# Norm scale and shift by two token tiles on GpSimd, and pieces of other work in any step

## The chip, the cores and the metric

The kernel runs on one core of one Trainium2 chip. A core has five engines that matter here: TensorE (matrix products; PE in the profile), VectorE (DVE), ScalarE (ACT), GpSimd (POOL), and SyncE (SP), which issues the transfers (DMA). Each engine works through its own queue of instructions in order and waits on semaphores for what others produce. The metric is the device time of one execution in microseconds (us), and lower is better.

## The reference, cut to what matters

Sixteen sequences of 1024 nodes with 128 features pass three graph transformer layers and then one graph attention layer. All share one 1024 x 1024 adjacency matrix.

```python
# layers 0 to 2, for each of 16 sequences
Q, K, V = x @ Wq, x @ Wk, x @ Wv                      # 8 heads of 16
scores = where(adj == 0, -inf, Q K^T / 4)             # 1024 x 1024 for each head
x = layer_norm(x + softmax(scores) V @ Wo + bo, ln1_g, ln1_b)
y = relu(x @ W1 + b1) @ W2 + b2                       # 128 -> 256 -> 128
x = layer_norm(x + y, ln2_g, ln2_b)
# layer 3
h = x @ W
e = leaky_relu((h @ a_src)[:, None] + (h @ a_dst)[None, :], 0.2)
out = layer_norm(softmax(where(adj == 0, -inf, e)) @ h + x, ln_gamma, ln_beta)
```

`layer_norm` ends in `... * g + b`: the scale and the shift that the change is about.

## The kernel before

The kernel handles 48 blocks (16 sequences by 3 layers), four sequences side by side, so that while one sequence's attention runs, the rest of another's layer is computed. A block has 32 steps: two groups of four heads, two halves of the queries, and eight tiles of keys (`kt`). A step computes the scores of four heads, as two pairs, against 128 keys; exponentiates and masks them; and four steps later (`AHEAD`) multiplies them with the values. One pair is always masked on VectorE, before the exponential (`mask_add`). The other is masked on GpSimd after it (`mask01`), except in the steps where `kt` is 2, 5 or 7: there VectorE masks both.

```python
LANES = 4
FEW = 20
AHEAD = 4
BOTH_ON_DVE = (2, 5, 7)
...
            on_pool = pp == 0 and kt not in BOTH_ON_DVE
            m = (mask01 if on_pool else mask_add)[:, kt, q0:q0 + 512][:, None, :].to_broadcast([P, 2, 512])
            if on_pool:
                nc.scalar.activation(ev, psv, AF.Exp, scale=HD ** -0.5)
                behind["pool"] = nc.gpsimd.tensor_mul(ev, ev, m).ins
            else:
                behind["dve"] = nc.vector.tensor_add(ev, psv, m).ins
                masked.append((2 * step_no[0] + pp + (kt not in BOTH_ON_DVE), ev))
```

All other work is cut into pieces. The projections of the next block are 8 pieces, what follows attention (output projection, norms, feed-forward) is 11, and the last layer of a sequence is 12. They stand in queues ("chains"), each with a least distance in steps from the piece ahead of it, and at most one is taken after a step, by `piece()`. `need(mark)` takes pieces at once until a given one is done.

```python
    def piece():
        few = sum(len(c["queue"]) for c in chains) < FEW and now[0] < (len(blocks) - LANES) * 4 * NT
        if few and now[0] % NT in BOTH_ON_DVE:
            return
        for chain in chains:
            if now[0] >= chain["due"] + chain["queue"][0][0] and take(chain):
                return
...
                if m + 1 < len(blocks):
                    if at == 6:
                        need(("post",) + (blocks[m + 1][0], blocks[m + 1][1] - 1) if blocks[m + 1][1] else
                             ("fetch", blocks[m + 1][0]))
                        put(proj_tasks(m + 1), ("proj", m + 1), first=True)
                    if at == 24:
                        need(("proj", m + 1))
                        stack(m + 1, 0)
```

`stack` copies keys and queries by DMA into the layout that the scores need. The norms: VectorE sums and takes the statistics (`stats`), and GpSimd normalises and then scales and shifts.

```python
    def normalise(n, ts):
        z, _, mv = n
        m, v = mv[:, ts, 0], mv[:, ts, 1]
        nc.gpsimd.tensor_scalar(m, m, -1.0, None, op0=OP.mult)
        nc.gpsimd.tensor_scalar(v, v, EPS, None, op0=OP.add)
        nc.gpsimd.tensor_tensor(v, v, half_neg[:, ts], OP.pow)
        for t in range(ts.start, ts.stop):
            nc.gpsimd.tensor_scalar(z[:, t, :], z[:, t, :], mv[:, t, 0:1], mv[:, t, 1:2], op0=OP.add, op1=OP.mult)

    def scale_shift(z, gain, bias):
        n = z.shape[1]
        nc.gpsimd.tensor_mul(z, z, rows(gain, n))
        nc.gpsimd.tensor_add(z, z, rows(bias, n))
```

When the half of the queries that is being summed ends, `finish` transposes the one accumulator on VectorE (`tt`), and GpSimd divides by the sums (`A`); the piece `both` transposes `A` on VectorE (`aT`).

```python
            with soon():
                nc.vector.transpose(tt.rearrange("p a b -> p (a b)"), acc)
            rec = state["recs"][:, g, qh, :]
            nc.vector.reciprocal(rec, tt[:, :, HD])
            nc.gpsimd.tensor_mul(state["A"][:, qh, :, g, :], tt[:, :, :HD],
                                 rec[:, :, None].to_broadcast([P, 16, HD]))
```

In the main loop the order on TensorE and ScalarE is that of the program; on VectorE and GpSimd a scheduler sets it when the kernel is built.

Of the kernel before, what the change touches and what calls it, by code (L numbers as in the profile page):

```python
# [28 lines left out]
SOON = 120  # L29
LANES = 4  # L30
FIRST = 1
FEW = 20
AHEAD = 4
BOTH_ON_DVE = (2, 5, 7)
TILES = {"w": 10, "x": LANES + 1, "last": 2}
# [77 lines left out]
def fast_path(ctx: ExitStack, tc: tile.TileContext, a: dict, out: bass.AP, flag):  # L113
    nc = tc.nc
    x_dram, adj = a["x"], a["adj"]
    B, N, D = x_dram.shape
    NT = N // P
# [40 lines left out]
    def fetch(b):  # L158
        def run():
            state["x", b] = load_x(b)  # L160
        return run
# [30 lines left out]
    def neighbours(t):  # L192
        ai, ab = rows_in[t]
        nc.vector.tensor_scalar(ab, ai, 0.0, None, op0=OP.not_equal)

    def mask_rows(t):
        ab = rows_in[t][1]
        ps = slot(BF16)
        for k in range(NT):
            nc.tensor.transpose(ps[:, k * P:(k + 1) * P], ab[:, k * P:(k + 1) * P], identb)  # L200
        return ps

    def masks(t, ps):
        psv = ps.rearrange("p (k q) -> p k q", q=P)
        nc.vector.tensor_copy(mask01[:, :, t * P:(t + 1) * P], psv)
        nc.scalar.activation(mask_add[:, :, t * P:(t + 1) * P], psv, AF.Identity, scale=-BLOCKED, bias=blocked,
                             saturate=False)
# [14 lines left out]
    def first_weights():  # L222
        W[0].update(load_layer(nc, nc.sync, const, a, 0, ("Wo", "b2", "W1", "b1", "W2", "ln1_g", "ln2_g")))
        norm_weights(nc.sync, 0)
# [5 lines left out]
    def other_weights():  # L230
        for l in range(1, L):
            W.append(load_layer(nc, nc.sync, const, a, l, [n for n in LAYER if n not in ("ln1_b", "ln2_b")]))
            norm_weights(nc.sync, l)
        nc.sync.dma_start(ln2_b_last, rows_of(a[f"L{L - 1}_gnn_ln2_b"]))
        for n in LAST:
            src = a[f"L3_gnn_{n}"]
            if n == "W":
                t = w_nodes[:, :D]
                nc.sync.dma_start(t, src)
            elif n in ("a_src", "a_dst"):  # L240
                t = const.tile([P, 1], F32, name=n)
                nc.sync.dma_start(t, src.rearrange("(p o) -> p o", o=1))
            else:
                t = const.tile([P, D], F32, name=n)
                nc.sync.dma_start(t, rows_of(src))
            wl[n] = t

    def biases():
        for l in range(L):
            if l:  # L250
                add_bias(nc.sync, "ln2_b", l - 1, "bo", l)
            add_bias(nc.sync, "ln1_b", l, "b2", l)

    def last_weights():
        a2 = const.tile([P, 2], F32)
        nc.vector.tensor_copy(a2[:, 0:1], wl["a_src"])
        nc.vector.tensor_copy(a2[:, 1:2], wl["a_dst"])
        ps = bank()
        nc.tensor.transpose(ps[:, :P], w_nodes[:, :D], identf)
        w3t = work.tile([P, P], F32, tag="row", name="w3t", bufs=2)  # L260
        nc.vector.tensor_copy(w3t, ps[:, :P])
        ps = bank()
        nc.tensor.matmul(ps[:, :2], w3t, a2, start=True, stop=True)
        nc.vector.tensor_copy(w_nodes[:, D:], ps[:, :2])
# [3 lines left out]
    for i in range(2):  # L268
        t = const.tile([P, NT, H, HD + 1], F32, name=f"v{i}")
# [29 lines left out]
    def rows(v, n=NT):  # L299
        return v[:, None, :].to_broadcast([P, n, D])  # L300
# [37 lines left out]
            nc.gpsimd.tensor_scalar(z[:, t, :], z[:, t, :], mv[:, t, 0:1], mv[:, t, 1:2], op0=OP.add, op1=OP.mult)  # L338

    def scale_shift(z, gain, bias):  # L340
        n = z.shape[1]
        nc.gpsimd.tensor_mul(z, z, rows(gain, n))  # L342
        nc.gpsimd.tensor_add(z, z, rows(bias, n))

    checks = [0]

# [51 lines left out]
    def stack(m, g):  # L398

        for pp in range(2):  # L400
            for n, order in (("Wk", (0, 1, 0, 1)), ("Wq", (0, 0, 1, 1))):
                t = work.tile([P, N], F32R, tag=n, name=n, bufs=4)
                r0 = (g * J + 2 * pp) * HD
                for i, part in enumerate(order):
                    behind["stack"] = nc.sync.dma_start(t[i:P:4, :].bitcast(F32), state[n, m][part][r0:r0 + 2 * HD, :].bitcast(F32)).ins
                state[n, g, pp] = t
# [245 lines left out]
    blocks = [(b, l) for p in range(0, B, LANES) for l in range(L) for b in range(p, p + LANES)]  # L652
    chains = []
    done = {("fetch", b) for b in range(2)}
    now = [0]
# [3 lines left out]
    def put(tasks, mark, chain=None, first=False):  # L659

        if chain is None:
            chain = {"due": now[0], "queue": deque()}
            chains.insert(0 if first else len(chains), chain)
        for n, task in enumerate(tasks):
            chain["queue"].append(task + (mark if n == len(tasks) - 1 else None,))
        return chain

    def take(chain):

        gap, f, tiles, mark = chain["queue"][0]  # L670
        if any(free[t[1:]] == 0 for t in tiles.split() if t[0] == "+"):
            return False
        chain["queue"].popleft()
        f()
        for t in tiles.split():
            free[t[1:]] += -1 if t[0] == "+" else 1
        done.add(mark)
        chain["due"] = now[0]
        if not chain["queue"]:
            chains.remove(chain)  # L680
        return True

    def piece():
        few = sum(len(c["queue"]) for c in chains) < FEW and now[0] < (len(blocks) - LANES) * 4 * NT
        if few and now[0] % NT in BOTH_ON_DVE:
            return
        for chain in chains:
            if now[0] >= chain["due"] + chain["queue"][0][0] and take(chain):
                return

    def need(mark):
        while mark not in done:
            first = next(c for c in chains if any(q[3] == mark for q in c["queue"]))
            assert take(first) or any(take(c) for c in list(chains) if c is not first)
# [62 lines left out]
    n = 0  # L757
    with tc.manual_schedule(engines={mybir.EngineType.PE, mybir.EngineType.Activation}):
        for m, (b, l) in enumerate(blocks):
            order = [(g, qh) for g in range(G) for qh in range(2)]  # L760
            if m in (0, len(blocks) - 1):
                order.sort(key=lambda x: x[1])
            for at, (g, qh, kt) in enumerate((g, qh, kt) for g, qh in order for kt in range(NT)):
                now[0] = n
                if at == (6 if m == 0 else 1):
                    stack(m, 1)
                if n == 6:
                    with tc.issue_after(behind["stack"]):
                        first_weights()
                        other_weights()  # L770
                if n == 20:
                    with tc.issue_after(behind["pool"]):
                        biases()
                if n == 40:
                    with tc.issue_after(behind["dve"]):
                        last_weights()
                if at == 0 and m + 2 < len(blocks) and blocks[m + 2][1] == 0:
                    put([(0, fetch(blocks[m + 2][0]), "+x")], ("fetch", blocks[m + 2][0]))
                if m + 1 < len(blocks):
                    if at == 6:  # L780
                        need(("post",) + (blocks[m + 1][0], blocks[m + 1][1] - 1) if blocks[m + 1][1] else
                             ("fetch", blocks[m + 1][0]))
                        put(proj_tasks(m + 1), ("proj", m + 1), first=True)
                    if at == 24:
                        need(("proj", m + 1))
                        stack(m + 1, 0)
                step = m, g, qh, kt
                if FIRST <= n < FIRST + 4:

                    with tc.manual_schedule(engines={mybir.EngineType.DVE}):  # L790
                        e = score_step(step)
                        neighbours(4 + n - FIRST)
                        masks(4 + n - FIRST, mask_rows(4 + n - FIRST))
                else:
                    e = score_step(step)
                waiting.append((step, e, n + AHEAD))
                av_due(n)
                piece()
                n += 1
        exponentials(0)  # L800
        for n in range(n, n + 2 * AHEAD):
            now[0] = n
            av_due(n)
            piece()
        while chains:
            now[0] += 1
            for chain in list(chains):
                if now[0] >= chain["due"] + chain["queue"][0][0]:
                    take(chain)
# [236 lines left out]
```

## Time and profile before

| | before |
|---|---|
| time, median of 3 | 4098.15 us (4097.01 to 4099.05) |
| span of the profiled execution | 4095.1 us |
| TensorE busy, granted clock | 3818.2 us, 0.98 |
| VectorE, ScalarE, GpSimd busy | 3393.5, 3381.9, 3450.5 us |
| GpSimd: mask product, 128 x 1024 (L428) | 960 of 2153 ns |
| GpSimd: scale, 128 x 1024 (L342) | 95 of 2394 ns |
| GpSimd: scale, 128 x 512 (L342) | 34 of some 1287 ns |

The profile shows one execution. Its page gives the busy time of each engine, the chain of work that ended last, and groups of instructions by source line. A group's row has the line, the engine, the operation, what it writes and reads, its shape and count, then its busy time in us and the mean of one in ns, then how long the engine idled just before it and what ended most of that. Busy times of engines that work side by side don't add up to the span.

### The profile page before, as it was taken

The numbers are of one execution on the slowest core, as the hardware profiler recorded it, in microseconds if no ns is written. First come the engines' busy times: TensorE is split into PE (matmuls) and PEld (weight loads), VectorE is DVE, ScalarE is ACT, GpSimd is POOL, SyncE is SP. The second block draws the span as 40 slices with busy tenths as digits, with TensorE's granted clock in tenths as the row PEclk, the third lists the DMA queues.
The fourth block names the chain that finished last, engine by engine and source line by source line (L and its number), as shares of the span: only waits on it lengthen the run. The fifth ranks groups of instructions, "written<-read, shape, count | busy, mean of one in ns | idle before, by whom it ended". The sixth has DMA issues, their size and how long they took to land.

```text
span 4095.1 us, 107716 instructions
## 1 busy us (share of the span) xinstructions
PE 3818.2 (93%) x44501; PEld 1548.0 (38%) x44501; DVE 3393.5 (83%) x5326; ACT 3381.9 (83%) x3961; POOL 3450.5 (84%) x3010
## 2 busy tenths in 40 slices
PE   7999999999999999999999999999999999999986
PEld 2333333344443333334444333333444433333445
DVE  7888888888788888888878888888888788888873
ACT  7999999977778999897777989998777798988760
POOL 5888988978878989898877989898887789998884
PEclk8999999999999999999999999999999999999997
DMA  6222122122222222122222222121222122221200
GB/s 160 61 63 58 47 63 63 42 62 54 58 54 63 50 63 63 43 64 54 53 54 62 54 63 59 46 63 43 74 54 54 48 63 52 54 63 42 62 12 17
DMA packets 124465, 233.13 MB, mean 57 GB/s; under 512 B 34624, under 2 KB 73792, under 8 KB 123968
## 3 DMA queue, kind: packets, MB, share of 16 engines
q1 hardware_dynamic: 122960, 225.71, 21.9%
q8 instruction: 354, 5.80, 0.6%
q14 instruction: 143, 1.17, 0.1%
q10 hardware_dynamic: 1008, 0.44, 0.1%
HBM read 15.54 MB, written 8.39 MB: 6 GB/s over the span
## 4 chain that ended last, share of the span: by engine, by line
PE 43%; DVE 21%; POOL 14%; ACT 14%; issue 6%; SPq 0%; DMA 0%; ACTq 0%; DVEq 0%; POOLq 0%
PE t L294 17%; PE acc L447 14%; DVE e L430 12%; PE s L420 11%; ACT e L442 7%; POOL e L428 7%; ACT e L427 4%; POOL x L338 3%; DVE st L319 2%; POOL mv L336 2%; DVE lo L383 2%; PE t L283 1%; DVE tt L458 1%; ACT hT L503 1%; POOL x L342 1%
## 5 line engine op out<-in xcount | busy, mean ns | idle before, releaser
L430 DVE TENSOR_TENSOR e<-s,mask_add 128x1024 f32<-128x1024 f32 x2112 | 2490.4, 1211 | 363.6 <-PE s L420 311.2
L442 ACT ACTIVATE e<-e 128x1024 f32<-128x1024 f32 x2112 | 2209.7, 1070 | 404.1 <-DVE e L430 385.0
L428 POOL TENSOR_TENSOR e<-e,mask 128x1024 f32<-128x1024 f32 x960 | 2052.8, 2153 | 322.7 <-ACT e L427 308.9
L447 PE MATMUL acc<-e,v 128*17 128x512 f32 x12288 | 1628.8, 602 | 49.4 <-DVE tt L458 22.2
L420 PE MATMUL s<-Wq,Wk 64*128 64x512 f32 x6144 | 1206.1, 459 | 90.1 <-DVE e L430 62.6
L427 ACT ACTIVATE e<-s 128x1024 f32<-128x1024 f32 x960 | 990.7, 1032 | 157.2 <-PE s L420 150.3
L420 PEld LDWEIGHTS s<-Wq,Wk 64*128 64x128 f32 x6144 | 501.6, 185 | 1078.1 <-DVE e L430 422.1
L447 PEld LDWEIGHTS acc<-e,v 128*17 128x17 f32 x12288 | 207.3, 95 | 556.4 <-issue 406.4
L338 POOL TENSOR_SCALAR x<-x,mv 128x128 f32<-128x128 f32 x896 | 392.3, 453 | 24.4
L294 PE MATMUL t<-hd,e 128*32 128x129 f32 x8192 | 253.7, 282 | 21.7 <-DVE lo L383 15.8
L342 POOL TENSOR_TENSOR x<-x,ln_g 128x1024 f32<-128x1024 f32 x97 | 230.0, 2371 | 32.0 <-PE t L283 31.7
L294 PEld LDWEIGHTS t<-hd,e 128*32 128x32 f32 x8192 | 234.9, 113 | 42.1 <-DVE lo L383 21.7
L336 POOL TENSOR_TENSOR mv<-mv,half_neg 128x4 f32<-128x4 f32 x224 | 232.6, 1038 | 18.5
L334 POOL TENSOR_SCALAR mv<-mv 128x4 f32<-128x4 f32 x224 | 53.1, 237 | 207.9 <-DVE mv L321 179.2
L326 DVE TENSOR_TENSOR x<-t,x 128x512 f32<-128x512 f32 x192 | 131.9, 687 | 112.8 <-PE t L294 110.4
L294 PE MATMUL t<-x1T,W 128*32 128x512 f32 x1536 | 205.1, 606 | 8.1 <-DVE lo L383 3.4
L294 PEld LDWEIGHTS t<-W,hT 128*32 128x32 f32 x6144 | 171.1, 111 | 75.6 <-issue 26.1
L319 DVE BATCH_NORM_STATS2 st<-x 128x6 f32<-128x128 f32 x896 | 196.0, 278 | 1.3
L294 PE MATMUL t<-W,hT 128*32 128x128 f32 x6144 | 189.3, 276 | 6.6 <-DVE lo L383 5.5
L283 PEld LDWEIGHTS t<-identf,x 128*128 128x128 f32 x888 | 95.0, 142 | 213.0 <-issue 64.1
L283 PE MATMUL t<-identf,x 128*128 128x128 f32 x888 | 149.1, 290 | 21.9 <-ACT xT L288 10.1
L383 DVE TENSOR_TENSOR lo<-t,hi 128x512 fp32r<-128x512 f32 x188 | 128.0, 681 | 32.9 <-ACT hi L382 32.5
(97 smaller groups left out, 2509.9 us busy)
## 6 DMA issues: line engine op xcount, KB each, us to landing
Wk<-hi SPq DMA_DIRECT2D x384, 128.0 KB
Wk<-lo SPq DMA_DIRECT2D x384, 128.0 KB
Wq<-hi SPq DMA_DIRECT2D x384, 128.0 KB
Wq<-lo SPq DMA_DIRECT2D x384, 128.0 KB
x<-in_x_dram SPq DMA_DIRECT2D x16, 512.0 KB
out_dram<-x SPq DMA_DIRECT2D x31, 256.0 KB
ai<-in_adj_dram SPq DMA_DIRECT2D x8, 512.0 KB
g_rows<-parts SPq DMA_DIRECT2D x120, 4.0 KB
```

What stands on the lines that cost most here:

```text
L283: nc.tensor.transpose(ps[:, t * P:(t + 1) * P], src[:, 4 * h + t, :], identf)
L294: nc.tensor.matmul(dst[j:j + SLOT, :], lhsT[:, j:j + SLOT], rhs, start=start, stop=stop)
L319: nc.vector.bn_stats(st[:, t, :], z[:, t, :])
L336: nc.gpsimd.tensor_tensor(v, v, half_neg[:, ts], OP.pow)
L338: nc.gpsimd.tensor_scalar(z[:, t, :], z[:, t, :], mv[:, t, 0:1], mv[:, t, 1:2], op0=OP.add, op1=OP.mult)
L342: nc.gpsimd.tensor_mul(z, z, rows(gain, n))
L420: nc.tensor.matmul(ps[:, r * 512:(r + 1) * 512], k[64 * r:64 * r + 64, kt * P:(kt + 1) * P], q[64 * r:64 * r + 64, q0:q0 + 512], start=Tru ...
L427: nc.scalar.activation(ev, psv, AF.Exp, scale=HD ** -0.5)
L428: behind["pool"] = nc.gpsimd.tensor_mul(ev, ev, m).ins
L430: behind["dve"] = nc.vector.tensor_add(ev, psv, m).ins
L442: nc.scalar.activation(ev, ev, AF.Exp, scale=HD ** -0.5)
L447: nc.tensor.matmul(acc[j * SLOT:j * SLOT + HD + 1, :], v_bufs[m % 2][:, kt, 2 * j + g, :], e[:, j, :], start=first, stop=last)
```

## The change

It has three parts. Scale and shift go by two token tiles (256 elements a partition) in place of all eight or four at once, so that a mask product on GpSimd can come between them. `piece()` loses its gate, so pieces may be taken in the steps in which VectorE masks both pairs too. And the first half of the next block's keys and queries is stacked at step 19 in place of 24, except in the first block.

```diff
-FEW = 20
...
     def scale_shift(z, gain, bias):
-        n = z.shape[1]
-        nc.gpsimd.tensor_mul(z, z, rows(gain, n))
-        nc.gpsimd.tensor_add(z, z, rows(bias, n))
+        for t in range(0, z.shape[1], 2):
+            nc.gpsimd.tensor_mul(z[:, t:t + 2, :], z[:, t:t + 2, :], rows(gain, 2))
+            nc.gpsimd.tensor_add(z[:, t:t + 2, :], z[:, t:t + 2, :], rows(bias, 2))
...
     def piece():
-        few = sum(len(c["queue"]) for c in chains) < FEW and now[0] < (len(blocks) - LANES) * 4 * NT
-        if few and now[0] % NT in BOTH_ON_DVE:
-            return
         for chain in chains:
...
-                    if at == 24:
+                    if at == (24 if m == 0 else 19):
                         need(("proj", m + 1))
                         stack(m + 1, 0)
```

## The prediction

> **What bounds the kernel now.** I read first the page's busy shares and its chain, then its costliest groups, then busy time by stretch, then TensorE's timeline.
>
> The page's shares, chain and groups:
>
> ```profile
> PE 3818.2 (93%) x44501; PEld 1548.0 (38%) x44501; DVE 3393.5 (83%) x5326; ACT 3381.9 (83%) x3961; POOL 3450.5 (84%) x3010
> ...
> PE 43%; DVE 21%; POOL 14%; ACT 14%; issue 6%; SPq 0%; DMA 0%; ACTq 0%; DVEq 0%; POOLq 0%
> ...
> L430 DVE TENSOR_TENSOR e<-s,mask_add 128x1024 f32<-128x1024 f32 x2112 | 2490.4, 1211 | 363.6 <-PE s L420 311.2
> L442 ACT ACTIVATE e<-e 128x1024 f32<-128x1024 f32 x2112 | 2209.7, 1070 | 404.1 <-DVE e L430 385.0
> L428 POOL TENSOR_TENSOR e<-e,mask 128x1024 f32<-128x1024 f32 x960 | 2052.8, 2153 | 322.7 <-ACT e L427 308.9
> L447 PE MATMUL acc<-e,v 128*17 128x512 f32 x12288 | 1628.8, 602 | 49.4 <-DVE tt L458 22.2
> ```
>
> TensorE is busy 93% of the span and idle for 4095.1 - 3818.2 = 277 us. Its largest named wait is small (the mask add on VectorE, 62.6 us of idle before the scores, in the group of L420). But the chain gives TensorE only 43%: four engines lie within 10 points of each other, so whichever gets more than its share of one stretch sets the pace there. What matters is how evenly the work is laid over the steps, and that is what the change touches.
>
> Busy time by stretch: block 18 (a "quiet" block: attention plus 19 pieces of other work, with the gate on), then block 45. In the last four blocks (44 to 47) the gate is already switched off by its own condition in the kernel before, so block 45 shows what ungated pieces do:
>
> ```profile
> core 0: us, PE busy (x) PEld busy (x) DVE busy (x) ACT busy (x) POOL busy (x), PEclk, DMA share, GB/s
> 1476.20:1550.70 74.50, 71.48 (x726) 25.43 (x722) 64.73 (x97) 68.97 (x79) 67.08 (x57) 1.00 0.24 58
> ...
> 3707.30:3789.00 81.70, 75.08 (x734) 26.87 (x730) 66.94 (x98) 70.81 (x80) 68.18 (x59) 0.96 0.22 53
> ```
>
> Gated, TensorE idles 74.5 - 71.5 = 3.0 us in a block; ungated 81.7 - 75.1 = 6.6 us, and its clock drops to 0.96. TensorE's timeline, first in block 18, then where block 44 passes into 45 and no piece stands for ten steps:
>
> ```profile
> 1482.23 1.05 PE L447 MATMUL acc<-e,v 128*17 128x512 f32 x8
> 1483.21 0.77 PE L420 MATMUL s<-Wq,Wk 64*128 64x512 f32 x4
> 1483.92 1.05 PE L447 MATMUL acc<-e,v 128*17 128x512 f32 x8
> 1484.79 1.04 PE L294 MATMUL t<-x1T,W 128*32 128x512 f32 x8
> ```
>
> ```profile
> 3701.02 1.05 PE L447 MATMUL acc<-e,v 128*17 128x512 f32 x8 [2.08 <-DVE tt L458]
> ...
> 3710.16 0.80 PE L420 MATMUL s<-Wq,Wk 64*128 64x512 f32 x2 [2.35 <-DVE e L430]
> 3710.89 1.91 PE L447 MATMUL acc<-e,v 128*17 128x512 f32 x8
> ```
>
> The distance of scores to scores is the length of a step: 1.65 us where TensorE has attention alone and nothing holds it, about 2.5 with one ordinary piece. In the second place TensorE stands twice for over 2 us, and after the second stop the value products take 1.91 in place of 1.05 us.
>
> **What the Trainium skill says.** "Perfetto Trace Analysis", section Identifying the Most-Contended Engine, warns that matmul busy time does not tell the distance from the roofline, and has one look for the gaps of the engine that should be saturated. The trace agrees that 93% tells little: the chain gives TensorE 43%. The same page, section Optimizing Scalar/DVE Operations, says that where engines are not saturated but cause bubbles elsewhere, breaking instructions up may let work finish sooner. That is the case for the two-tile form; here TensorE idles only 19.6 us for GpSimd's mask product. "GPSIMD Engine Reference", section 3.1, puts a two-input elementwise operation at about 2.6 cycles an element at 1.2 GHz (2.17 ns) plus a dispatch per instruction. The trace agrees: 2391 ns for 1024 elements and 1287 ns for 512 give 2.16 ns an element and 183 ns fixed.
>
> **Part 1, scale and shift by two tiles.** An instruction over 256 elements then costs 183 + 256 x 2.16 = 735 ns (estimate). There are 95 products and 95 additions over 1024 (2.39 us each), and 34 and 34 over 512 (1.29 us). Each long one becomes four: 4 x 0.735 - 2.39 = +0.55 us, times 190 = +104 us. Each short one becomes two: +0.18 us, times 68 = +12 us. GpSimd's busy time goes from 3450 to about 3565 us (87%), in a quiet block from 67.1 by 2.2 to some 69.3 of 75 us. All that is off TensorE's path as long as a mask product ends before its value product, four steps (about 10 us) later. The finer pieces let a mask slip in between, but in the built program's GpSimd order they also stand earlier: after the mask of step 6 come five of these short ones and a whole normalisation (0.24 + 0.23 + 1.04 + 1.75 = 3.3 us), about 7 us ahead of the mask of step 8, two steps (5 us) later. I count 0 to +15 us on the path.
>
> **Part 2, stack at step 19.** The copies of the next block's keys and queries start five steps (some 12 us) earlier. No matmul of a quiet block waits for a DMA in the trace, so it saves nothing: 0. (With the gate on, three projections would have had to be forced into one step for this; without it they end at step 18.)
>
> **Part 3, the gate goes.** I followed the queue's rule over all 1536 steps; it has no times in it. Before, 205 of 1077 pieces taken inside the loop fall into steps where VectorE masks both pairs (kt 2, 5, 7); after, 429. The number of steps without matmul work beside attention hardly moves: 532 before, 525 after. But their place does. Before, 304 of them stand alone between steps with pieces, and such a step takes 1.71 us on average. After, a quiet block takes its 19 pieces in steps 5 to 25 and leaves steps 26 to 31 and 0 to 4 of the next empty: 26 runs of about twelve.
>
> In a long run the buffers (three score slots, four steps of lag) can't carry TensorE ahead at 1.65 us, since ScalarE has two exponentials a step, which start 0.94 us apart back to back (two in a row show as 1.99): 1.88 us. The trace has runs of four to six empty steps, and they take 2.10 to 2.21 us a step. For a quiet block after the change:
> - Steps 5 to 25: block 45 has the same pieces at the same steps, and takes 54.6 us for them.
> - The eleven other steps: 11 x 1.88 = 20.7 us at ScalarE's pace, 11 x 2.1 = 23.1 at the pace of the runs seen.
> - Together 75.3 to 77.7 us, middle 76.5. The quiet blocks take 73.1 to 77.7 us now, 75.3 on average. That is +1.2 us (0 to +2.4) in each of 26 such blocks (1 to 8, 15 to 20, 27 to 32, 39 to 44): +31 us (0 to +62).
>
> The stop of 2.35 us at block 45 is not counted. It came from VectorE's transpose of A standing in its queue ahead of three mask adds while GpSimd was late; in the new order it stands three adds later. In the busy blocks (9 to 14, 21 to 26, 33 to 38; 80 to 101 us) the queue mostly held 20 or more, so the gate was mostly open: 0, give or take 15. As a second way I gave each step after the change the mean time, in the trace of before, of a step with the same kind of piece and the same kind of masking. The sum is +78 us, which is too much where it charges short runs at a mean that holds long ones. Between +31 and +78, with some of Part 1, I take +45.
>
> **Sum:** 4098 + 45 = 4143 us.
>
> **Rivals.**
> 1. *Pieces in double-mask steps overload VectorE at once.* There it has two adds already (2.26 us in a row), so a piece with 0.69 + 0.86 + 0.36 us more (sum and statistics) exceeds the step. For it: one such step of block 45 took 3.59 us. Against it: in the open stretches a feed-forward piece takes a median of 2.51 us in those steps and 2.54 in the others; the slots absorb it. If it held for each of the 224 pieces moved, at 0.5 us, the time would be about 4210.
> 2. *Finer GpSimd work and an even queue win.* Pieces pile up less (queue at a busy block's start 21 in place of 24 at most), and forced pieces go from 37 to 6. If the busy blocks' idle of 5 to 8 us fell by 2 in each of 18, and quiet blocks ran at ScalarE's pace, the time would be about 4065. Against it: their long steps are edge and aggregate pieces (6 to 9.9 us), which stay.
> 3. *GpSimd becomes the bound.* With 69.3 of 75 us and bursts of 7 us it holds the value products. At 1 us a block: about 4190.
>
> **Range and chances.** The quiet blocks alone give 0 to +62, GpSimd 0 to +15, busy blocks -15 to +15: 4090 to 4195 holds it eight times in ten. For 2% faster (4016) more than a quarter of TensorE's idle would have to vanish: 0.03. For 2% slower (4180) rival 1 or 3 must add to mine: 0.17.
>
> **What would show it.** In the changed profile: quiet blocks near 76.5 us with 71.5 of TensorE busy; TensorE's idle up by 30 to 60 us, most of it in steps 26 to 31 and 0 to 4; steps 5 to 25 near 54.6 us; 256-element products near 735 ns; GpSimd near 3565 us busy; no new wait for DMA. I am wrong if quiet blocks fall under 74.5, if value products wait for GpSimd by tens of us, or if busy blocks move by more than 3 us each.

## The result, and the profile after

| | before | after |
|---|---|---|
| time, median of 4 runs each | 4097.74 us | 4135.98 us (4131.86 to 4141.88) |
| ratio, 95% interval | | 1.0094 [1.0077, 1.0112] |
| span of the profiled execution | 4095.1 us | 4140.1 us |
| TensorE idle in it (span less busy) | 277 us | 319 us |
| GpSimd busy | 3450.5 us | 3539.4 us |

The change makes the kernel about 0.9% slower, 38 us by the medians; 4143 us was predicted. Its four executions took 4131.9 us twice, 4140.1 and 4141.9; the profile shows the longest, whose span is 45.0 us over that of the kernel before. The page of the changed kernel, shares, chain and groups as shown of the kernel before (line numbers here are one lower), and the row of the new short scale:

```profile
PE 3820.8 (92%) x44501; PEld 1548.2 (37%) x44501; DVE 3405.0 (82%) x5326; ACT 3396.4 (82%) x3961; POOL 3539.4 (85%) x3648
...
PE 46%; DVE 20%; POOL 12%; ACT 12%; issue 8%; SPq 1%; DMA 0%; ACTq 0%; DVEq 0%; POOLq 0%
...
L429 DVE TENSOR_TENSOR e<-s,mask_add 128x1024 f32<-128x1024 f32 x2112 | 2499.3, 1211 | 418.8 <-PE s L419 307.7
L441 ACT ACTIVATE e<-e 128x1024 f32<-128x1024 f32 x2112 | 2196.8, 1063 | 368.9 <-DVE e L429 341.7
L427 POOL TENSOR_TENSOR e<-e,mask 128x1024 f32<-128x1024 f32 x960 | 2052.9, 2154 | 388.1 <-ACT e L426 378.5
L446 PE MATMUL acc<-e,v 128*17 128x512 f32 x12288 | 1631.7, 603 | 66.0 <-DVE tt L457 31.9
...
L341 POOL TENSOR_TENSOR x<-x,ln_g 128x256 f32<-128x256 f32 x384 | 277.6, 741 | 21.0 <-PE t L282 21.0
```

The page hardly tells the two kernels apart: the operations kept their lengths, TensorE's busy time is the same within 3 us, and only idle time grew, over many small waits (the value products idle 66.0 us in place of 49.4). One has to go by block. The distance between the first score matmuls of successive blocks, added up in the two traces:

| blocks | before | after |
|---|---|---|
| 26 quiet blocks (1 to 8, 15 to 20, 27 to 32, 39 to 44) | 1964.4 us | +38.9 us |
| TensorE idle in them | 93.8 us | +37.2 us |
| 18 busy blocks (9 to 14, 21 to 26, 33 to 38) | 1641.3 us | +9.0 us |
| the rest of the span | 489.4 us | -2.9 us |

So most of the loss lies in the quiet blocks and is idle time of TensorE. The +9.0 us of the busy blocks may belong to this one execution: in the trace of the changed kernel with the stack at step 24 (e4 below, a shorter execution) they take 1.6 us less than before.

A step lasts from its first score matmul to that of the next. The 832 steps of the quiet blocks, sorted by whether TensorE has anything but attention in them, in the two traces:

| steps of the 26 quiet blocks | before | after |
|---|---|---|
| empty (attention alone) | 356 steps, 658.3 us, 1.85 each | 361 steps, 700.6 us, 1.94 each |
| with a piece | 476 steps, 1306.2 us, 2.74 each | 471 steps, 1302.7 us, 2.77 each |

By length, all of the loss is in the empty steps, though their number hardly moved. Before, 212 of them stood alone between two steps with pieces and took 1.67 us each; the other 144 took 2.12. After, 309 of 361 stand in runs, at 1.93 us.

Busy time by stretch in the changed kernel: block 18, then its steps 5 to 25 alone, then the eleven empty steps that follow (columns as in the prediction):

```profile
1499.68:1576.15 76.47, 71.64 (x724) 25.62 (x721) 65.36 (x97) 69.50 (x79) 68.85 (x69) 1.00 0.23 57
1509.30:1564.39 55.09, 51.77 (x592) 20.23 (x588) 44.64 (x69) 49.68 (x59) 49.13 (x48) 1.00 0.19 46
1564.39:1585.76 21.37, 19.87 (x136) 5.39 (x132) 20.70 (x28) 19.81 (x21) 19.74 (x22) 1.00 0.37 93
```

In the third stretch VectorE is busy 20.70 of 21.37 us (97%), ScalarE and GpSimd 93% and 92%, and a step takes 1.94 us on average. TensorE's timeline at the start of such a stretch, changed kernel:

```profile
1566.04 0.94 PE L419 MATMUL s<-Wq,Wk 64*128 64x512 f32 x4
1566.91 1.05 PE L446 MATMUL acc<-e,v 128*17 128x512 f32 x8
1568.48 0.74 PE L419 MATMUL s<-Wq,Wk 64*128 64x512 f32 x4 [0.52 <-ACT e L426]
1569.36 1.05 PE L446 MATMUL acc<-e,v 128*17 128x512 f32 x8
```

From scores to scores it is 2.44 us here, without a piece between them, where TensorE alone would need 1.65: the scores wait for a slot that ScalarE's exponential gives back. Over the whole span this wait of the scores rises from 9.1 to 34.5 us (the waits of TensorE, before and after):

```profile
PE s L420 <- ACT e L427: 9.1, 29, 0.5
```

```profile
PE s L419 <- ACT e L426: 34.5, 105, 0.6
```

### The profile page after: what moved, and what is told of

It is laid out like the page before. It is cut to its first block, busy times and chain, and to the rows that moved or that the text cites. A ratio compares the mean times of both kernels' runs of the same rounds, so it can differ in the third digit from the quotient of the medians.

```text
span 4140.1 us, 108453 instructions
## 1 busy us (share of the span) xinstructions
PE 3820.8 (92%) x44501; PEld 1548.2 (37%) x44501; DVE 3405.0 (82%) x5326; ACT 3396.4 (82%) x3961; POOL 3539.4 (85%) x3648
## 4 chain that ended last, share of the span: by engine, by line
PE 46%; DVE 20%; POOL 12%; ACT 12%; issue 8%; SPq 1%; DMA 0%; ACTq 0%; DVEq 0%; POOLq 0%
PE t L293 18%; PE acc L446 15%; PE s L419 11%; DVE e L429 11%; POOL e L427 7%; ACT e L441 5%; ACT e L426 5%; DVE st L318 2%; PE t L282 2%; POOL x L337 2%; DVE x L325 2%; DVE lo L382 1%; ACT xT L287 1%; DVE tt L457 1%; POOL mv L335 1%
## 5 line engine op out<-in xcount | busy, mean ns | idle before, releaser
L419 PE MATMUL s<-Wq,Wk 64*128 64x512 f32 x6144 | 1210.7, 459 | 84.5 <-ACT e L426 34.5
L341 POOL TENSOR_TENSOR x<-x,ln_g 128x256 f32<-128x256 f32 x384 | 277.6, 741 | 21.0 <-PE t L282 21.0
L293 PE MATMUL t<-hd,e 128*32 128x129 f32 x8192 | 243.8, 276 | 4.8 <-DVE x L621 3.4
L293 PEld LDWEIGHTS t<-hd,e 128*32 128x32 f32 x8192 | 226.6, 111 | 23.5 <-DVE x L325 5.1
L606 DVE SCALAR_TENSOR_TENSOR e<-s,mask 128x1024 f32<-128x1024 f32 x128 | 150.5, 1209 | 4.8 <-PE s L603 3.9
```

What stands on the lines that cost most here:

```text
L293: nc.tensor.matmul(dst[j:j + SLOT, :], lhsT[:, j:j + SLOT], rhs, start=start, stop=stop)
L341: nc.gpsimd.tensor_mul(z[:, t:t + 2, :], z[:, t:t + 2, :], rows(gain, 2))
L419: nc.tensor.matmul(ps[:, r * 512:(r + 1) * 512], k[64 * r:64 * r + 64, kt * P:(kt + 1) * P], q[64 * r:64 * r + 64, q0:q0 + 512], start=Tru ...
```

## The experiments

All ratios are to the kernel before, run on the same chip. **My theory** at the outset: the gate's removal costs about 31 us because the empty steps now stand in long runs, paced by ScalarE; the two-tile form costs 0 to 15 us; the stack at step 19 nothing. **Rival 1:** pieces in steps where VectorE masks both pairs overload VectorE. **Rival 3:** the short GpSimd instructions hold the value products up.

### The three parts, one by one

`e1_gate_off`, the kernel before without its gate:

```diff
-        few = sum(len(c["queue"]) for c in chains) < FEW and now[0] < (len(blocks) - LANES) * 4 * NT
-        if few and now[0] % NT in BOTH_ON_DVE:
-            return
```

> Kernel before with the gate alone taken out (stack at step 24, scale and shift whole). My theory, that the place of the empty steps costs the time: 4125 to 4145 us, quiet blocks near 76.2 us. If the short GpSimd instructions cost it: 4095 to 4108 us.

Measured: 4119.73 us, ratio 1.0050 [1.0036, 1.0064].

`e2_two_tiles`, the kernel before with the two-tile form:

```diff
-        nc.gpsimd.tensor_mul(z, z, rows(gain, n))
-        nc.gpsimd.tensor_add(z, z, rows(bias, n))
+        for t in range(0, z.shape[1], 2):
+            nc.gpsimd.tensor_mul(z[:, t:t + 2, :], z[:, t:t + 2, :], rows(gain, 2))
+            nc.gpsimd.tensor_add(z[:, t:t + 2, :], z[:, t:t + 2, :], rows(bias, 2))
```

> Kernel before with scale and shift by two tiles alone (gate kept, stack at 24). My theory: 4095 to 4113 us, GpSimd busy some 90 us more, quiet blocks unchanged within 0.5 us. If the short GpSimd instructions cost the time: 4120 to 4140 us.

Measured: 4120.21 us, ratio 1.0055 [1.0041, 1.0068].

`e3_after_whole`, the changed kernel with scale and shift whole:

```diff
-        for t in range(0, z.shape[1], 2):
-            nc.gpsimd.tensor_mul(z[:, t:t + 2, :], z[:, t:t + 2, :], rows(gain, 2))
-            nc.gpsimd.tensor_add(z[:, t:t + 2, :], z[:, t:t + 2, :], rows(bias, 2))
+        n = z.shape[1]
+        nc.gpsimd.tensor_mul(z, z, rows(gain, n))
+        nc.gpsimd.tensor_add(z, z, rows(bias, n))
```

> Changed kernel with scale and shift whole again (no gate, stack at 19). My theory: 4121 to 4136 us, at most 15 us under the changed kernel. If the finer pieces help where there is no gate: 4140 to 4160 us.

Measured: 4123.42 us, ratio 1.0061 [1.0047, 1.0075].

`e4_after_24`, the changed kernel with the stack at step 24:

```diff
-                    if at == (24 if m == 0 else 19):
+                    if at == 24:
```

> Changed kernel with the stack at step 24 again. My theory: 4132 to 4141 us, as the changed kernel, since no step waits for these copies. If the early copies gain: 4145 us or more; if they cost: 4130 us or less.

Measured: 4132.32 us, ratio 1.0083 [1.0069, 1.0096].

What follows. The gate alone costs 0.50% (some 20 us, which leaves e1 5 us under the range I gave for it), the two-tile form alone 0.55% (some 23 us). The latter is more than my upper end of 15 and just inside what was written for e2 if the short instructions cost the time, so about half of the loss of the single parts is the two-tile form's. Together (e4) they cost 0.83%, less than their sum. Without a gate the two-tile form costs 0.33% (e4 less e1, and again after less e3). The stack's step can't be told from nothing: e3 and e1, and after and e4, lie 0.11% apart with overlapping intervals.

In e1's trace the quiet blocks of the steady state take 76.1 us, as I said (76.2), and the loop from block 1 to 46 takes 3811.5 us in place of 3783.6: +27.9, close to the 31 of the prediction. Block 47 with the tail after it took 202.7 us in place of 209.9, which gives 7 back. TensorE's work there is the same, but its granted clock in the tail was 0.82 in place of 0.77. In the traces without a gate and with whole scale and shift (e1, e3) this last part takes 202.7 and 202.0 us, in the changed kernel, e2 and e4 208.9 to 214.9.

### Where the two-tile form loses

In e2's trace, 19.4 us longer than that of the kernel before, 20 of the 22 quiet blocks that follow another quiet block stand within 0.6 us of the kernel before (block 16 takes 1.9 us more, block 44 0.9), but blocks 15, 27 and 39 take 4.2 us more each (80.8 in place of 76.6), 12.6 us together; block 47 with the tail takes 5.0 more. GpSimd's timeline in block 27, first the kernel before, then e2:

```profile
2262.16 2.41 POOL L342 TENSOR_TENSOR x<-x,ln_g 128x1024 f32<-128x1024 f32 x1
2264.51 2.17 POOL L428 TENSOR_TENSOR e<-e,mask 128x1024 f32<-128x1024 f32 x1
```

```profile
2268.49 0.73 POOL L343 TENSOR_TENSOR x<-x,b 128x256 f32<-128x256 f32 x1
2269.18 0.73 POOL L342 TENSOR_TENSOR x<-x,ln_g 128x256 f32<-128x256 f32 x1
2269.88 0.62 POOL L461 TENSOR_TENSOR A<-tt,recs 128x256 f32<-128x256 f32 x1
2270.45 0.74 POOL L343 TENSOR_TENSOR x<-x,b 128x256 f32<-128x256 f32 x1
2271.15 1.43 POOL L342 TENSOR_TENSOR x<-x,ln_g 128x256 f32<-128x256 f32 x2
2272.55 2.12 POOL L428 TENSOR_TENSOR e<-e,mask 128x1024 f32<-128x1024 f32 x1
```

Before, one scale stands ahead of the mask product. In e2 five short ones and the division stand there, over 4 us. The form was meant to let masks in between; here the scheduler used the finer grain to put more of it ahead of a mask. TensorE in e2, at the same place:

```profile
2271.74 0.73 PE L420 MATMUL s<-Wq,Wk 64*128 64x512 f32 x4
2274.72 1.08 PE L447 MATMUL acc<-e,v 128*17 128x512 f32 x8 [2.25 <-POOL e L428]
2275.73 1.12 PE L283 MATMUL t<-identf,x 128*128 128x128 f32 x4
2276.78 1.22 PE L420 MATMUL s<-Wq,Wk 64*128 64x512 f32 x4
2277.93 1.57 PE L447 MATMUL acc<-e,v 128*17 128x512 f32 x8
```

The value product waits 2.25 us for that mask, and the matmuls after it run slower (1.57 in place of 1.05 us for the eight), so the stop costs more than itself: in block 27 TensorE is busy for 73.92 us in place of 71.43, at a granted clock of 0.96 in place of 1.00, which is 2.5 of the 4.2 us. Over the whole span TensorE's waits for the mask product rise from 19.6 to 40.8 us (the waits of TensorE, before and e2):

```profile
PE acc L447 <- POOL e L428: 19.6, 29, 2.6
```

```profile
PE acc L447 <- POOL e L428: 40.8, 35, 2.6
```

In the changed kernel the form costs something else. Blocks 15, 27 and 39 take 81.7 to 82.1 us there and 81.6 to 81.9 with scale and shift whole (e3), so this stop adds nothing without the gate. Of the 12.4 us between the traces of e4 and e1, which differ in the form alone, 5.1 lie in the quiet blocks, 1.1 in the busy ones and 6.2 in block 47 with the tail. Why stays open.

`e12_halves` cuts the same work in two but lays the halves into two steps, each where its half is transposed (shown for one of three places):

```diff
-                    if h == 1:
-                        scale_shift(x, W[l - 1]["ln2_g"], w["bo"])
+                    scale_shift(x[:, 4 * h:4 * h + 4, :], W[l - 1]["ln2_g"], w["bo"])
```

> Kernel before with scale and shift in two halves of four tiles, each in the step that transposes its half, so the GpSimd work is cut in two but also laid into two steps. If it is the burst of short instructions ahead of a mask that makes the two-tile form slow: 4088 to 4104 us, no value product waits 2 us for GpSimd. If it is their number (about a third of the extra time): 4103 to 4110.

Measured: 4103.99 us, ratio 1.0014 [1.0006, 1.0023], where the two expectations meet. Its wait on the mask product is 24.8 us, the longest 1.7, and GpSimd is busy 3475.0 us. So finer pieces laid over two steps cost little, but they gain nothing either. Both their number and their place differ from e2, so this doesn't tell which of the two makes the two-tile form slow.

### Spread alone, or the right steps

`e5_gate_036` keeps a gate that spreads the empty steps as before, but closes it in other steps, so that pieces go where VectorE masks both pairs:

```diff
-        if few and now[0] % NT in BOTH_ON_DVE:
+        if few and now[0] % NT in (0, 3, 6):
```

> Kernel before with its gate on steps with kt 0, 3, 6 in place of 2, 5, 7: the empty steps still stand alone, but 531 pieces in place of 205 fall into steps where VectorE masks both pairs. My theory (how the empty steps are spread decides): 4090 to 4115 us. Rival 1 (a piece in such a step overloads VectorE): 4140 to 4210 us.

Measured: 4306.15 us, ratio 1.0504 [1.0486, 1.0521]. My theory in that form falls: the lone empty steps do take 1.65 us each (steps 11, 14, 16 and so on of block 18), but the quiet blocks take 82.4 us, since the steps with pieces lengthen: their sum is 1490.3 us in place of 1306.2 in the kernel before, that of the empty steps 652.8 in place of 658.3. VectorE's and TensorE's timelines in e5, block 19, steps 12 and 13:

```profile
1692.06 1.23 DVE L430 TENSOR_TENSOR e<-s,mask_add 128x1024 f32<-128x1024 f32 x1 [1.26 <-PE s L420]
1693.20 0.68 DVE L383 TENSOR_TENSOR lo<-t,hi 128x512 fp32r<-128x512 f32 x1
```

```profile
1689.68 1.05 PE L447 MATMUL acc<-e,v 128*17 128x512 f32 x8 [0.82 <-DVE tt L458]
...
1694.03 1.08 PE L294 MATMUL t<-Wo,aT 128*32 128x128 f32 x32 [0.79 <-DVE lo L383]
```

TensorE waits for a VectorE that idled 1.26 us just before: the work comes in heaps, two adds and a piece in one step and a single add in the next. So Rival 1 holds here. Against the kernel before, 531 - 205 = 326 more pieces lie in such steps, at 208 / 326 = 0.64 us each. In the changed kernel 224 more lie there, and steps 5 to 25 show no such price. I take it that the dense pieces around them, at 2.6 us a step (54.8 / 21), give VectorE the time to catch up; that was not tested. The gate of the kernel before did two things, then: it spread the empty steps, and it put them where VectorE has two adds. e5 changed the second and kept the first; no run changes the first alone.

### What paces a long run of empty steps

I added a small operation in each of the steps 26 to 31 and 0 to 4 of the changed kernel, on one engine at a time. On ScalarE (`e6_dose_act`):

```diff
+                if n > 40 and (at > 25 or at < 5):
+                    nc.scalar.copy(dose_out, dose_in)
```

> Changed kernel with one extra ScalarE copy of 256 elements (some 0.3 us) in each of the eleven empty steps 26 to 31 and 0 to 4, about 510 in all. My theory (ScalarE sets the pace of these steps): those of the 26 quiet blocks lengthen by most of the dose, +60 to +100 us, 4195 to 4235. If VectorE or GpSimd sets it: under +30 us.

Measured: 4173.62 us, ratio 1.0181 [1.0164, 1.0198]. The time rose by about 36 us over the changed kernel, between the two expectations, and a quiet block by 1.35 us (77.63 in place of 76.28, the average of the 21 that follow a quiet block while the gate of the kernel before is on: 2 to 8, 16 to 20, 28 to 32, 40 to 43). The copy takes 399 ns, so eleven are 4.4 us by their length. But copy and exponential overlap: ScalarE's busy time in such a block rises from 69.61 to 72.35 us, by 2.74. Of this, 1.35 us lengthen the block and 1.38 go into idle time that ScalarE had elsewhere in it. "Most of the dose" left that idle time out. The delay shows in steps 5 to 25 (+1.0 us) and 26 to 31 (+0.5), in steps 0 to 4 not at all.

The same operation on VectorE and GpSimd (`e7_dose_dve`, `e8_dose_pool`) tells nothing. It had no tie to its step, and the scheduler, which orders these two engines, moved it ahead, into the first 1084 us in e7 and the first 366 in e8:

```diff
+                    nc.vector.tensor_tensor(dose_out, dose_in, dose_in, OP.mult)            # e7
+                    nc.gpsimd.tensor_scalar(dose_out[:, 0], identf, 2.0, None, op0=OP.mult)   # e8
```

> Changed kernel with one extra VectorE product of 256 elements (some 0.3 us) in each of the same steps. My theory: under +40 us, since VectorE has 1.55 us of adds a step against ScalarE's 1.88. If VectorE sets the pace: +60 to +100 us.

> Changed kernel with one extra GpSimd operation of 128 elements (some 0.43 us) in each of the same steps. My theory: under +20 us, since GpSimd has 1.3 us of mask products a step there. If GpSimd sets the pace: +80 us or more.

Measured: 4378.83 us, ratio 1.0682 [1.0664, 1.0700], and 4393.37 us, ratio 1.0721 [1.0703, 1.0739]. In e8 block 0 took 331 us in place of 82, in e7 blocks 0 to 10 were longer, and the later ones took what they take without the dose: nearly all of the loss came from work in the wrong place.

`e9_more_dve` and `e10_more_pool` tie the extra work to its step by doing part of the mask twice, which leaves the values the same:

```diff
+                if long_run and pp:
+                    nc.vector.tensor_add(ev[:, 0, :256], psv[:, 0, :256], m[:, 0, :256])      # e9
+                if long_run:
+                    nc.gpsimd.tensor_mul(ev[:, 0, :128], ev[:, 0, :128], m[:, 0, :128])       # e10
```

> Changed kernel; in the eleven steps 26 to 31 and 0 to 4 of a block VectorE's mask add is done once more over 256 columns before the whole one (same values, some 0.35 us a step, bound to its step by its data). If VectorE paces these steps beside ScalarE: +1.5 us or more in a quiet block, 4170 to 4220 us in all. If ScalarE alone does: under +0.5 us a block, 4136 to 4155.

> Changed kernel; in the same eleven steps GpSimd's mask product is done once more over 128 columns (mask of 0 and 1, same values, some 0.45 us in seven of the steps). My theory, GpSimd has time to spare there: under +0.5 us in a quiet block, 4130 to 4150 us. If GpSimd paces these steps: 4180 us or more.

Measured: e9 4331.71 us, ratio 1.0569 [1.0553, 1.0586]; e10 4162.77 us, ratio 1.0158 [1.0143, 1.0174].

e9 looks like proof that VectorE sets the pace, and is none. On average over the same 21 quiet blocks its steps 0 to 4 take 9.55 us (9.60 in the changed kernel), for five extra adds of 405 ns; its steps 26 to 31 take 18.36 in place of 11.85. VectorE's timeline there, in e9:

```profile
1654.15 0.36 DVE L431 TENSOR_TENSOR e<-s,mask_add 128x256 f32<-128x256 f32 x1
1657.79 0.71 DVE L476 STREAM_TRANSPOSE aT<-A 128x512 f32<-128x512 f32 x1 [3.29 <-POOL A L463]
1658.43 2.32 DVE L432 TENSOR_TENSOR e<-s,mask_add 128x1024 f32<-128x1024 f32 x2
```

The extra adds made the scheduler put the transpose of A ahead of two mask adds, while GpSimd had not yet made A. The queue stood 3.29 us, TensorE with it. It is the stop that the prediction saw at the start of block 45, now in the midst of quiet blocks. In e10 the quiet blocks stay as they were (76.34 us on average, 76.28 in the changed kernel), so GpSimd doesn't pace the runs; the cost came in the busy blocks and the ones just after them. TensorE's wait for the mask product is 69.9 us there, 28.9 in the changed kernel.

In steps 0 to 4 none of the three extra loads lengthened the five steps by more than 0.4 us, so these runs alone don't name the engine that sets the pace. The profile of the changed kernel says more. Steps 0 to 4 of block 19, columns as in the prediction:

```profile
1576.15:1585.76 9.61, 9.04 (x64) 2.40 (x60) 9.15 (x9) 9.61 (x11) 8.66 (x6) 1.00 0.78 200
```

ScalarE is busy for all of the 9.61 us. Its 17 exponentials that start from 1574.59 to 1589.53 us stand 0.93 us apart, which is 1.87 us for the two of a step, the floor that the prediction gave. VectorE took five extra adds of 405 ns in these steps (e9), and they became no longer. The six steps ahead, 26 to 31 of block 18, are different: ScalarE idles for 1.56 of 11.76 us there, 1.24 of them before an exponential that waits for a mask add, and VectorE is busy for 11.55. So the second half of a long run goes at ScalarE's pace. In the first half ScalarE waits for a VectorE that is busy nearly all the time; that this is left over from the pieces just ahead is argued, not tested.

### An attempt to beat both

`e11_edges_single`: in the kernel before, the first edges-and-aggregate piece took over 8 us in six of nine cases in steps with two masks on VectorE.

```diff
+            if now[0] % NT in BOTH_ON_DVE and getattr(chain["queue"][0][1], "heavy", False):
+                continue
```

> Kernel before; the three pieces of the last layer that hold edges and an aggregate may not be taken in steps where VectorE masks both pairs. In the kernel before, the first of them takes 8.5 us in such a step and 6.3 in others, nine times. If VectorE's load in these steps is the cause: 4075 to 4092 us, under both kernels. If it is the piece itself: 4095 to 4110.

Measured: 4113.36 us, ratio 1.0041 [1.0027, 1.0054]. The pieces did what was hoped: the first one takes 6.2 us on average in place of 8.5 for those nine. But later pieces shifted with it. The busy blocks came out even (+0.5 us), quiet ones together 16 us longer, and block 47 with the tail 5. In the changed kernel the same pieces take 6.0 us in steps with two masks, so the kind of step was not the cause. In the kernel before, TensorE waits 2.36 us in the middle of one for a projection's remainder (`lo`), which stands behind the edges in VectorE's queue. None of the twelve kernels is faster than the one before.

## Why the prediction was right

- **The time**: 4143 predicted, 4136 measured, range 4090 to 4195. The sum is right within 7 us, partly by luck: the terms are not all so.
- **Part 3, the gate**: the two halves of a quiet block came as worked out: steps 5 to 25 take 54.8 us (54.6), the other eleven 21.4 (20.7 to 23.1), the block 76.2 where nothing disturbs it (76.5). Over the 26 blocks that is +38.9 us with all parts and +34.0 with the gate alone, against +31 (0 to +62). The average of 75.3 us before left block 44 out, with which it is 75.6. The 38.9 us are not all the predicted effect, though. The 21 blocks named at e6 rise by 22.6 (1.1 each, 1.2 predicted); block 1 and the first blocks after the busy stretches (15, 27, 39) rise by 22.4, which the prediction did not go into, and block 44, ungated before as well, falls by 6.1.
- **The reason given for the pace of the empty steps was half right.** "ScalarE has two exponentials a step" gave 1.88 us as a floor. In steps 0 to 4, ScalarE without a gap goes at 1.87; in steps 26 to 31, at 1.98 us a step, it waits for VectorE. The average of 1.94 lies between the floor and the 2.1 of the short runs seen before.
- **A sign that did not come**: TensorE's idle time was to grow mostly in steps 26 to 31 and 0 to 4. In the quiet blocks it went there from 44.5 to 42.0 us, and in steps 5 to 25 from 49.2 to 88.9. Of this, 26.7 us are one stop of 1.0 us a block at step 16, where a transposition waits for a projection's remainder (`lo`); before, no transposition of a quiet block waited for it. Idle time by place and the length of steps by kind are two measures of one loss and don't agree here; the prediction worked with the second and named the first as its sign.
- **Part 1, two tiles**: "0 to +15 us on the path" was too small: +23 us with the gate, +13 without. The mechanism was named (short instructions and their place in the built order), but I counted only the seven microseconds ahead of one mask in a quiet block. I did not go through the blocks after a busy stretch (15, 27, 39), where with the gate the stop of 2.25 us arose, nor the tail; where the 13 without a gate come from is open. The instruction's length was right (741 ns, 735 estimated). GpSimd's busy time rose by 89 us and not 115: two in a row take 1.43 us, not 1.48.
- **Part 2, the stack**: nothing, as said, within what the runs can tell.
- **Busy blocks**: +9.0 us in the profiled execution, inside the 15 either way; single ones moved by -8 to +12 us, which I had named as a sign of being wrong, and which cancelled.
- **Rival 1** was set aside on the right ground for this change, the equal lengths of feed-forward pieces in both kinds of step, but e5 shows it is real where the lighter steps stand empty. **Rival 2** fell: no part gains. **Rival 3** is not what came, since e10's extra GpSimd work left the quiet blocks as they were, but a wait for GpSimd, in three blocks, is most of what the two-tile form costs with the gate. The second way, means by kind of step, gave +78 and was too high, among other things because it charged the first edges piece with stops of the old schedule (8.5 us in steps with two masks, 6.0 in the changed kernel).

## What to carry to other kernels

Where four engines are nearly even, count in which steps side work lands, not only how much of it there is: empty steps are cheap one at a time, at the place where another engine has its heaviest load (1.67 us here, 1.93 to 2.12 in runs). When a scheduler orders an engine, read the built order before believing that smaller instructions let others in between; it may put more of them ahead. And a kernel of before can hold its own experiment: the blocks in which a condition already switched the gate off gave the prediction its best number.

## What was not expected of the hardware

A stop of TensorE of some 2 us can be followed by slower matmuls, but need not be. In the traces eight value products took 1.57 us in e2 and 1.91 in e9 and in the kernel before, in place of 1.05, up to 4 us after a stop of 2.25 to 3.28 us; yet after the stop of 2.08 us that the prediction shows they took 1.05. Of the 11 stops of 1.9 us and more between blocks 1 and 46 of the kernel before, 3 have a group of over 1.5 us among the next four groups of value products, in the changed kernel 9 of 13. And in the tail, where TensorE stops and goes, the same work took 112.6 us at a granted clock of 0.82 in e1 and 119.7 us at 0.77 in the kernel before.
